# A block-sparse layer, two gated feed-forwards and a state-space mixer on one core: another order for the mask of the first stage and for the last phase of the mixer

## The chip, the core and the metric

The kernel runs on one core of a Trainium2 chip, as one launch. A core has a matrix engine (TensorE, PE in the profile, whose loads of stationary operands have a row of their own, PEld), VectorE (DVE), ScalarE (ACT), GpSimd (POOL) and SyncE (SP), which here only issues DMA transfers. Each engine works through its own list of instructions in order and waits for the others by semaphores. The metric is the device time of one execution in microseconds; lower is better.

## What is computed

1024 tokens (2 sequences of 512) of width 512, in float32, go through four residual layers. In each, `x` is normalised first:

```python
x = x + attn_a(layernorm(x), mask, weight, bias)      # block-sparse linear layer
x = x + ffn(layernorm(x), gate, up, down)             # integer weights, dequantised
x = x + attn_b(layernorm(x), in_proj, conv, ...)      # state-space mixer, 128 heads
x = x + ffn(layernorm(x), gate, up, down)

# attn_a: a block of 32x32 weights counts if any entry of its mask is set
bm  = mask.reshape(16, 32, 16, 32).sum(axis=(1, 3)) > 0
w   = (weight.reshape(16, 32, 16, 32) * bm[:, None, :, None]).reshape(512, 512)
out = einsum('bsk,nk->bsn', data, w) + bias

# attn_b, its end: y of all 8192 channels is normalised, gated and projected
var = mean(square(y), axis=-1)
y   = y * rsqrt(var + eps) * norm_w * silu(gate)
return y @ out_proj_w.T
```

Of the rest of the mixer only this matters here: a projection of each token into gates, channels and scores, a short convolution, a scan over chunks of 128 tokens, and the projection above.

## The kernel before

**Layout.** Tokens lie in 8 tiles of 128 (`x_sb[:, t, :]`, token on the partition, 512 wide). The normalised and turned input `xn_t` has the width on the partition, in 4 chunks `kc` of 128. `norm(t, True)` (line 110) issues the statistics of tile `t` (two VectorE instructions, L115 and L117) and a square root on ScalarE (L119); it returns a function which, called later, does the reciprocal and the offset on VectorE (L122, L126) and writes the normalised tile `tmp` on ScalarE (L127). `turn` (line 137) transposes such a tile by four TensorE instructions and copies it into `xn_t` on ScalarE (L143).

**Who sets the order.** `tc.manual_schedule` (line 1537) takes TensorE, ScalarE and VectorE as they stand in the code: what is written first runs first. The lists of POOL and SP are put in order by a planner from dependencies, priorities and its own estimates.

**First stage** (`block_sparse`, line 290). The weight comes in four chunks `wt[:, kc]` and the mask in four chunks `mk[:, kc]`. `masked(kc)` (line 322) is a generator in two parts. The look-up sums the mask over 32 columns on VectorE (`rows`, L325) and over 32 rows on TensorE, by a product with a block matrix (`pb`, L327). The masking compares that with zero on VectorE (`on`, L330) and multiplies the chunk of weights by it (L333), on VectorE for chunks 0 to 2 and on POOL for chunk 3. After some 20 warming products (`stir`), tiles 0 and 1 are normalised and turned, and their products run chunk by chunk in alternation (lines 358 to 364) with the look-up and the masking of the next chunk between them. The loop after that (line 371) takes tile after tile: POOL adds the bias to `x` (L372), TensorE multiplies, VectorE adds the product to `x` (L383), and the tile is normalised for the feed-forward.

**Mixer.** It works through the 8192 channels in 32 phases of two tiles of 128 channels. Each phase's projection is added into `acc`, which shares its memory with `x_sb`; the input is kept in DRAM (`x_d`) and read back into `xr`. Squares of `y` are summed into `sq_acc` by `squares` (line 947): ScalarE squares, POOL adds.

**Last phase** (lines 1456 to 1533). It finishes the scores and scans of the last two channel tiles and interleaves the start of the second feed-forward. `back_scores(k)` makes one set of scores (ScalarE and POOL); `flush` does the waiting multiplies by `gm` on VectorE (L900); `half_scan(units[2:], "proj")` is the TensorE part of the scan for the second sequence and `finish` its two VectorE instructions per channel tile (`y`, L939; `gt`, L942). `last_outs(t)` projects token tile `t`: four TensorE instructions (L956) and an addition on VectorE (L968), at once for tiles 0 to 3 and put off to the end (`adds`) for tiles 4 to 7. Tiles 0 to 3 need the first sequence alone; tiles 4 to 7 need `gt` of the second. `factors(b)` sums the squares of a sequence over the partitions on TensorE (`ms`, L1421) and forms the factor `rn` (L107, L108). `rest(t)` (line 1445) is `residual(t)`, which forms `acc * rn + xr` in one VectorE instruction (L1441), followed by `norm(t, True)`. Before the change, `ahead(t)` (line 1494) issues `rest(t + 1)` and then the normalised tile `t`. The second feed-forward starts with `pg` and `pu` (L486), which read all four turned tiles of the first sequence.

Of the kernel before, what the change touches and what calls it, by code (L numbers as in the profile page):

```python
# [11 lines left out]
ALU = mybir.AluOpType  # L12
AX = mybir.AxisListType

P = 128
# [5 lines left out]
KC = DIM // P  # L21
# [16 lines left out]
def kernel(  # L38
# [25 lines left out]
    nc = tc.nc  # L64
# [72 lines left out]
    def turn(normed):  # L137

        t, xn = normed
        pt = psum.tile([P, KC, P], F32, tag="tr", name="ln_tr")  # L140
        for kc in range(KC):
            nc.tensor.transpose(pt[:, kc, :], xn[:, kc * P : (kc + 1) * P], ident)
        nc.scalar.copy(xn_t[:, :, t * P : (t + 1) * P], pt)  # L143
# [85 lines left out]
    def stir(n):  # L229

        ps = psum.tile([P, P], F32, tag="tr", name="stir")
        for _ in range(n):
            nc.tensor.matmul(ps, lhsT=ones, rhs=ones, start=True, stop=True)
# [44 lines left out]
    def now(q_compute):  # L278
        q, compute = q_compute
        compute()  # L280
        return q

    def dequant_gate(s, scratch, third=False):
        return dequant_in(s, gate_w, gate_z, gate_s, scratch, third)

    def dequant_up(s, scratch, third=False):
        return dequant_in(s, up_w, up_z, up_s, scratch, third)


    def block_sparse():  # L290

        with tc.tile_pool(name="bs", bufs=1) as pool:

            def scratch(shape):
                return [pool.tile(shape, ty, name=nm, bufs=2) for nm, ty in (("wi", I32), ("zi", I32), ("sf", F32))]

            wt = pool.tile([P, KC, DIM], F32, name="wt")
            mk = pool.tile([P, KC, DIM], I32, name="mk")
            bias_b = pool.tile([P, DIM], F32, name="bias_b")

            def load_x(t):
                nc.sync.dma_start(x_sb[:, t, :], x_in[t * P : (t + 1) * P, :])

            for t in range(2):
                load_x(t)
            for kc in range(KC):
                nc.scalar.dma_start(mk[:, kc], mask_t[kc * P : (kc + 1) * P, :])
                nc.sync.dma_start(wt[:, kc], w_t[kc * P : (kc + 1) * P, :])

            nc.scalar.activation(small.tile([P, 1], F32, name="root"), eps, AF.Sqrt)  # L310
            for t in range(2, 5):
                load_x(t)
            nc.sync.dma_start(bias_b, bias.to_broadcast([P, DIM]))
            for t in range(5, NT):
                load_x(t)
            bd = pool.tile([P, P], F32, name="bd")
            nc.vector.memset(bd, 0.0)
            for i in range(4):
                nc.vector.memset(bd[32 * i : 32 * i + 32, 32 * i : 32 * i + 32], 1.0)
            NB = DIM // 32  # L320

            def masked(kc):

                rows = pool.tile([P, NB], F32, name="rows", bufs=2)
                nc.vector.tensor_reduce(rows, mk[:, kc].rearrange("p (b j) -> p b j", j=32), AX.X, ALU.add)  # L325
                pb = psum.tile([P, NB], F32, tag="yo", name="pb", bufs=3)
                nc.tensor.matmul(pb, lhsT=bd, rhs=rows, start=True, stop=True)  # L327
                yield
                on = pool.tile([P, NB], F32, name="on", bufs=2)
                nc.vector.tensor_scalar(on, pb, 0.0, None, ALU.is_gt)  # L330
                wv = wt[:, kc].rearrange("p (b j) -> p b j", j=32)
                eng = nc.gpsimd if kc == KC - 1 else nc.vector
                eng.tensor_tensor(wv, wv, on.unsqueeze(2).to_broadcast([P, NB, 32]), ALU.mult)  # L333
                yield

            def product(t, po, kc):
                nc.tensor.matmul(
                    po,
                    lhsT=xn_t[:, kc, t * P : (t + 1) * P],
                    rhs=wt[:, kc, :],  # L340
                    start=(kc == 0),
                    stop=(kc == KC - 1),
                )

            def bs_o():
                return psum.tile([P, DIM], F32, tag="proj", name="bs_o", bufs=3)


            stir(20)
            mask = [masked(kc) for kc in range(KC)]  # L350
            halves = [norm(t, True) for t in range(2)]
            normed = [h() for h in halves]
            next(mask[0])
            for n in normed:
                turn(n)
            next(mask[0])
            pos = [bs_o() for _ in range(2)]
            for kc in range(KC):
                product(0, pos[0], kc)
                if kc + 1 < KC:  # L360
                    next(mask[kc + 1])
                product(1, pos[1], kc)
                if kc + 1 < KC:
                    next(mask[kc + 1])
            ahead = norm(2, True)()
            half = norm(3, True)
            waiting = []
            half_f = None
            loaded = [dequant_gate(0, scratch), dequant_up(0, scratch)]
            first = []  # L370
            for t in range(NT):
                nc.gpsimd.tensor_add(x_sb[:, t, :], x_sb[:, t, :], bias_b)  # L372
                if t < 2:
                    po = pos[t]
                else:
                    po = bs_o()
                    for kc in range(KC):
                        product(t, po, kc)
                if t + 2 < NT:
                    turn(ahead)  # L380
                if t + 3 < NT:
                    ahead = half()
                nc.vector.tensor_add(x_sb[:, t, :], x_sb[:, t, :], po)  # L383
                if t + 4 < NT:
                    half = norm(t + 4, True)
                if half_f:
                    waiting.append(half_f())
                half_f = norm(t, True)
                if t in (4, 5):
                    first.append(now(loaded.pop(0)))  # L390
                if len(waiting) == 2:
                    turn(waiting.pop(0))
            waiting.append(half_f())
        return first, [lambda n=n: lambda: turn(n) for n in waiting]
# [274 lines left out]
    def mixer(waiting, step_args, loaded):  # L669

        with ExitStack() as st:
# [206 lines left out]
            def flush():  # L878
                for f in mults:
                    f()  # L880
                mults.clear()
# [274 lines left out]
            for ph in range(1, n_ph + 1):  # L1156
# [19 lines left out]
                def all_squares():  # L1176
                    for b, y in ys:
                        squares(b, y)
                    ys.clear()
# [9 lines left out]
                def back_scores(k):  # L1189
                    half_scores(k, c1, heads)  # L1190
# [227 lines left out]
            def factors(b):  # L1418
                ms = psum.tile([P, NCH], F32, tag="tr", name="ms")
                for c in range(NCH):  # L1420
                    nc.tensor.matmul(  # L1421
                        ms[:, c : c + 1],
                        lhsT=sq_acc[:, b, c * P : (c + 1) * P],
                        rhs=ones[:, 0:1],
                        start=True,
                        stop=True,
                    )
                rsqrt(rn[:, b * NCH : (b + 1) * NCH], ms, 1.0 / INTER)
# [16 lines left out]
            def rest(t):  # L1445
                residual(t)
                return norm(t, True)
# [3 lines left out]
            def last_outs(t):  # L1451

                tag = "proj" if t in (4, 6, 7) else "yo"
                out_project(n_ph - 1, [t], gts, wo_last, tag, None if t < NCH else adds)
# [31 lines left out]
            flush()  # L1486
            last_outs(1)
            back_scores(7)
            factors(0)
            last_outs(2)  # L1490
            flush()
            half = rest(0)

            def ahead(t):

                nonlocal half
                new = rest(t + 1)
                normed = half()
                half = new
                return normed  # L1500

            scans = half_scan(units[2:], "proj")
            normed = ahead(0)
            finish(scans)
            last_outs(3)
            turn(normed)
            normed = ahead(1)
            last_outs(4)
            turn(normed)
            normed = ahead(2)  # L1510
            last_outs(5)
            all_squares()
            turn(normed)
            normed = half()
            last_outs(6)
            turn(normed)
            last_outs(7)
            for f in adds:
                f()
            factors(1)  # L1520
# [3 lines left out]
            half = norm(NCH)  # L1524
# [101 lines left out]
```

## Time and profile before

| | us |
|---|---|
| median of 3 runs | 2304.89 (2302.44 to 2306.73) |
| the profiled execution, its own time | 2304.02 |
| its span, first to last instruction | 2302.3 |
| first stage, to the first product of the feed-forward (`pg`) | 0 to 47.4 |
| first feed-forward | 47.4 to about 314 |
| mixer | about 314 to 2039.6 |
| of it: last phase, from its first transposes | 1991.7 to 2039.6 |
| second feed-forward | 2039.6 to 2302.3 |

The profile is of one execution. "Busy" is time in which an engine works on an instruction; TensorE's instructions are pipelined and their ends are modelled, so that starts of successive ones say more than lengths. The chain of waits follows the work that ended last backwards to what released each step. Idle time of an engine that does not set the end costs nothing.

### The profile page before, as it was taken

The numbers are of one execution on the slowest core, as the hardware profiler recorded it, in microseconds if no ns is written. First come the engines' busy times: TensorE is split into PE (matmuls) and PEld (weight loads), VectorE is DVE, ScalarE is ACT, GpSimd is POOL, SyncE is SP. The second block draws the span as 40 slices with busy tenths as digits, with TensorE's granted clock in tenths as the row PEclk, the third lists the DMA queues.
The fourth block names the chain that finished last, engine by engine and source line by source line (L and its number), as shares of the span: only waits on it lengthen the run. The fifth ranks groups of instructions, "written<-read, shape, count | busy, mean of one in ns | idle before, by whom it ended". The sixth has DMA issues, their size and how long they took to land.

```text
span 2302.3 us, 30183 instructions
## 1 busy us (share of the span) xinstructions
PE 2242.4 (97%) x10704; PEld 1411.4 (61%) x10704; DVE 1805.7 (78%) x3042; ACT 1180.2 (51%) x2532; POOL 1243.9 (54%) x1206
## 2 busy tenths in 40 slices
PE   9999999999999999999999999999999999999999
PEld 5445865656665666666566656666666665544468
DVE  5456568888888888888888888888888888865553
ACT  4111056756666665666566656656655666631100
POOL 3765024656655666566556555664665665527620
PEclk9999999999999999999999999999999999999999
DMA  5563021222222222222221222221222322326600
GB/s 188 191 199 105 28 74 55 74 74 65 73 74 65 74 85 71 74 74 74 64 74 65 77 68 75 74 83 58 81 75 63 110 65 74 119 83 223 201 24 28
DMA packets 145783, 201.59 MB, mean 88 GB/s; under 512 B 7136, under 2 KB 92000, under 8 KB 145632
## 3 DMA queue, kind: packets, MB, share of 16 engines
q1 hardware_dynamic: 145056, 198.61, 27.1%
q8 instruction: 85, 1.39, 0.3%
q10 hardware_dynamic: 576, 1.05, 0.1%
q14 instruction: 66, 0.54, 0.1%
HBM read 194.91 MB, written 4.72 MB: 87 GB/s over the span
## 4 chain that ended last, share of the span: by engine, by line
PE 83%; DVE 14%; issue 2%; ACT 1%; DMA 1%; POOL 0%; ACTq 0%; SPq 0%; POOLq 0%; DVEq 0%
PE proj L185 29%; PE yo L185 17%; PE po L1020 10%; PE ffn_o L556 7%; DVE m L900 5%; DVE x_sb L1034 5%; PE py L919 4%; PE pst L848 4%; PE py L928 3%; PE x_tr L827 2%; PE po L956 2%; DVE gt L942 1%; PE pg L486 1%; PE pu L486 1%; DVE xc L734 1%
## 5 line engine op out<-in xcount | busy, mean ns | idle before, releaser
L906 POOL TENSOR_TENSOR ce<-ce,c_t 128x384 f32<-128x384 f32 x256 | 267.7, 1051 | 340.7 <-ACT ce L902 335.0
L185 PE MATMUL proj<-xn_t,w 128*128 128x512 f32 x824 | 384.6, 593 | 2.0 <-DVE gt L206 1.7
L892 ACT ACTIVATE m<-bc,acs 128x128 f32<-128x128 f32 x1024 | 324.9, 390 | 4.4 <-PE py L919 4.4
L185 PEld LDWEIGHTS proj<-xn_t,w 128*128 128x128 f32 x824 | 153.0, 190 | 146.4 <-issue 137.7
L1034 DVE TENSOR_TENSOR x_sb<-x_sb,po 128x512 f32<-128x512 f32 x340 | 228.9, 679 | 9.5 <-PE po L1020 4.9
L171 POOL TENSOR_TENSOR ws<-w 128x256 f32<-128x256 f32 x96 | 72.9, 760 | 292.2 <-DMA w<-in_win_t_dram 242.1
L734 DVE SCALAR_TENSOR_TENSOR xc<-proj,cw,xc 128x511 f32<-128x511 f32 (+2 forms) x288 | 214.6, 746 | 6.6
L900 DVE TENSOR_TENSOR m<-m,gm 128x512 f32<-128x512 f32 x256 | 218.6, 876 | 0.0
L919 PE MATMUL py<-m,x_dt 128*64 128x128 f32 x2048 | 194.1, 278 | 13.7 <-DVE m L900 13.6
L949 POOL TENSOR_TENSOR sq_acc<-sq_acc,y 128x512 f32<-128x512 f32 x128 | 178.4, 1400 | 46.5 <-ACT y L948 43.8
L185 PE MATMUL proj<-tq,ws 128*128 128x512 f32 x432 | 199.2, 592 | 0.0
L1020 PE MATMUL po<-wo,gt 128*128 128x256 f32 x696 | 177.0, 384 | 0.0
L919 PEld LDWEIGHTS py<-m,x_dt 128*64 128x64 f32 x2048 | 135.8, 137 | 49.0 <-issue 25.8
L899 ACT ACTIVATE m<-m 128x512 f32<-128x512 f32 x256 | 161.3, 630 | 7.4
L185 PE MATMUL yo<-xn_t,w 128*128 128x512 f32 x328 | 151.7, 595 | 12.8 <-DVE tmp L206 12.8
L928 PE MATMUL py<-ce,state 128*64 128x128 f32 x1536 | 157.6, 274 | 0.0
L862 DVE SCALAR_TENSOR_TENSOR state<-state,e_last,pst 128x64 f32<-128x64 f32 x512 | 107.0, 276 | 60.2 <-ACT state L857 57.7
L185 PE MATMUL yo<-tq,ws 128*128 128x512 f32 x336 | 153.4, 599 | 0.2 <-ACT acs L714 0.2
L1020 PEld LDWEIGHTS po<-wo,gt 128*128 128x128 f32 x696 | 125.5, 190 | 30.9 <-issue 7.1
L749 ACT ACTIVATE xc<-xc 128x512 f32<-128x512 f32 x128 | 72.5, 621 | 134.3 <-DVE xc L734 133.9
L731 ACT ACTIVATE xc<-proj,cb,cw 128x512 f32<-128x512 f32 x96 | 74.4, 778 | 129.5 <-DVE proj L225 76.6
L942 DVE SCALAR_TENSOR_TENSOR gt<-y,nw,gt 128x512 f32<-128x512 f32 x128 | 137.1, 1071 | 2.5
(228 smaller groups left out, 4559.5 us busy)
## 6 DMA issues: line engine op xcount, KB each, us to landing
bc<-acs_d SPq DMA_DIRECT2D x128, 512.0 KB, 3.8
w<-in_win_t_dram SPq DMA_DIRECT2D x64, 512.0 KB, 3.8
wo<-in_wo_t_dram SPq DMA_DIRECT2D x31, 512.0 KB, 5.0
wi<-in_down_w_dram SPq DMA_DIRECT2D x14, 512.0 KB, 4.0
zi<-in_down_z_dram SPq DMA_DIRECT2D x14, 512.0 KB, 4.8
sf<-in_down_s_dram SPq DMA_DIRECT2D x14, 512.0 KB, 4.2
wi<-in_gate_w_dram SPq DMA_DIRECT2D x13, 512.0 KB, 4.3
zi<-in_gate_z_dram SPq DMA_DIRECT2D x13, 512.0 KB, 5.2
```

Source lines behind the costliest of these rows:

```text
L185: nc.tensor.matmul(ps, lhsT=a[:, kc, :], rhs=b[:, kc, :], start=(start and kc == 0), stop=(stop and kc == KH - 1), skip_group_check=True,)
L556: nc.tensor.matmul(ps, lhsT=a[:, k, :], rhs=b(k), start=(start and k == 0), stop=(stop and k == KF - 1), skip_group_check=True,)
L734: nc.vector.scalar_tensor_tensor(dst[:, s:], ps[:, : SEQ - s], cw[:, t, 3 - s : 4 - s], dst[:, s:], ALU.mult, ALU.add)
L892: nc.scalar.activation(m[:, c, :], bc[:, hh, c * P : (c + 1) * P], AF.Relu, bias=acs[:, t, h : h + 1], scale=-1.0,)
L899: nc.scalar.activation(m, m, AF.Exp, scale=-1.0)
L900: mults.append(lambda: nc.vector.tensor_mul(m, m, shared[b][2]))
L906: nc.gpsimd.tensor_mul(ce, ce, c_t[:, P:].rearrange("p (c l) -> p c l", l=P))
L919: nc.tensor.matmul(py[hh * HD : (hh + 1) * HD, c * P : (c + 1) * P], lhsT=x_dt[:, c, hh, :], rhs=m[:, c, :], start=True, stop=(c == 0),)
L928: nc.tensor.matmul(py[hh * HD : (hh + 1) * HD, c * P : (c + 1) * P], lhsT=state[:, c - 1, hh, :], rhs=ce[:, c - 1, :], start=False, stop=True,
L949: nc.gpsimd.tensor_add(sq_acc[:, b, :], sq_acc[:, b, :], y)
L1020: nc.tensor.matmul(banks[k][:, c, :], lhsT=a[:, t], rhs=b, start=(start and c == 0), stop=stop, skip_group_check=True,)
L1034: nc.vector.tensor_add(q, q, banks[k])
```

## The change

In the first stage, the look-ups of chunks 0 and 1 are issued ahead of the turns of tiles 0 and 1, and that of chunk `kc + 2` ahead of the products of chunk `kc`; the maskings stay between the two products of the chunk before. The masking of chunk 3 is done by VectorE like the others.

In the last phase, the waiting multiply (`flush`) and `rest(0)` come ahead of the projection of tile 2, `rest(1)` stays behind the issue of the scan; the normalised tile 1 is written ahead of the residuals of tiles 2 and 3; the squares come ahead of the projection of tile 4; the two residuals are issued together, ahead of the projection of tile 5; and the turns of tiles 1, 2 and 3 each stand one projection later than before.

```diff
@@ -329,8 +329,7 @@
                 on = pool.tile([P, NB], F32, name="on", bufs=2)
                 nc.vector.tensor_scalar(on, pb, 0.0, None, ALU.is_gt)
                 wv = wt[:, kc].rearrange("p (b j) -> p b j", j=32)
-                eng = nc.gpsimd if kc == KC - 1 else nc.vector
-                eng.tensor_tensor(wv, wv, on.unsqueeze(2).to_broadcast([P, NB, 32]), ALU.mult)
+                nc.vector.tensor_tensor(wv, wv, on.unsqueeze(2).to_broadcast([P, NB, 32]), ALU.mult)
                 yield
 
             def product(t, po, kc):
@@ -350,18 +349,20 @@
             mask = [masked(kc) for kc in range(KC)]
             halves = [norm(t, True) for t in range(2)]
             normed = [h() for h in halves]
+
             next(mask[0])
+            next(mask[1])
             for n in normed:
                 turn(n)
             next(mask[0])
             pos = [bs_o() for _ in range(2)]
             for kc in range(KC):
+                if kc + 2 < KC:
+                    next(mask[kc + 2])
                 product(0, pos[0], kc)
                 if kc + 1 < KC:
                     next(mask[kc + 1])
                 product(1, pos[1], kc)
-                if kc + 1 < KC:
-                    next(mask[kc + 1])
             ahead = norm(2, True)()
             half = norm(3, True)
             waiting = []
@@ -1486,35 +1487,27 @@
             flush()
             last_outs(1)
             back_scores(7)
+            flush()
             factors(0)
+            first_rest = rest(0)
             last_outs(2)
-            flush()
-            half = rest(0)
-
-            def ahead(t):
-
-                nonlocal half
-                new = rest(t + 1)
-                normed = half()
-                half = new
-                return normed
-
             scans = half_scan(units[2:], "proj")
-            normed = ahead(0)
+            second_rest = rest(1)
+            normed = first_rest()
             finish(scans)
             last_outs(3)
             turn(normed)
-            normed = ahead(1)
+            normed = second_rest()
+            all_squares()
             last_outs(4)
+            halves = [rest(2), rest(3)]
+            last_outs(5)
             turn(normed)
-            normed = ahead(2)
-            last_outs(5)
-            all_squares()
-            turn(normed)
-            normed = half()
+            normed = [h() for h in halves]
             last_outs(6)
-            turn(normed)
+            turn(normed[0])
             last_outs(7)
+            turn(normed[1])
             for f in adds:
                 f()
             factors(1)
```

## The prediction, made before the changed kernel was run

> **What bounds the kernel now.** First the page's busy row and its chain, for the bound of the whole; then the chain of waits and the timeline in the two stretches that the change touches, 8 to 23 us and 2016 to 2040 us; then the windows, for the granted clock there.
>
> ```profile
> PE 2242.4 (97%) x10704; PEld 1411.4 (61%) x10704; DVE 1805.7 (78%) x3042; ACT 1180.2 (51%) x2532; POOL 1243.9 (54%) x1206
> PE 83%; DVE 14%; issue 2%; ACT 1%; DMA 1%; POOL 0%; ACTq 0%; SPq 0%; POOLq 0%; DVEq 0%
> ```
>
> TensorE is the bound, and its order is written by hand. So what is worth anything is time in which PE stands still, and a stall removed early should reach the end unless a later wait hangs on something other than PE. The first stretch, as a timeline (start, length, engine, line, operation; in brackets the idle before and who ended it):
>
> ```profile
> 14.60 2.49 POOL L372 TENSOR_TENSOR x_sb<-x_sb,bias_b 128x512 f32<-128x512 f32 x2 [12.61 <-DMA bias_b<-in_bias_dram]
> ...
> 17.04 1.05 POOL L333 TENSOR_TENSOR wt<-wt,on 128x512 f32<-128x512 f32 x1
> ...
> 18.14 0.30 PEld L337 LDWEIGHTS bs_o<-wt,xn_t 128*128 128x128 f32 x2 [2.48 <-POOL wt L333]
> ```
>
> The masking of the last chunk runs on POOL behind two bias additions, which wait for the bias (landed at 14.43). Its look-up was done at 15.75; PE has it at 18.14. The earlier chunks stall PE too: the look-up's reduction, PE sum, comparison and multiply of a chunk follow each other between two products. The last phase, as the chain of waits (start, length, what):
>
> ```profile
> 2027.15 0.60 DVE x_sb L968
> 2027.74 0.67 DVE x_sb L1441
> 2028.44 0.70 DVE stats L115
> 2029.17 0.18 DVE mv L117
> 2029.35 0.06 DVE rstd L122
> 2029.43 0.23 DVE off L126
> 2029.66 0.03 issue
> 2029.68 0.82 ACT tmp L127
> 2030.51 0.04 issue
> 2030.55 0.98 PE ln_tr L142 x4
> 2031.53 3.08 PE po L956 x4
> ```
>
> PE ran out at 2028.06 and waits 2.5 us for VectorE to do tile 2's residual and statistics and only then tile 1's scale, because each normalised tile is written one step after its statistics. The last two rows are too long (0.98 for four transposes that take 0.44 elsewhere, 3.08 for products that take 1.72), and the windows of half a microsecond say why (length, busy of PE, PEld, DVE, ACT, POOL, then the granted clock):
>
> ```profile
> 2030.00:2030.50 0.50, 0.00 (x0) 0.00 (x0) 0.47 (x2) 0.50 (x1) 0.00 (x0) 1.00 0.00 0
> 2030.50:2031.00 0.50, 0.45 (x3) 0.45 (x4) 0.50 (x1) 0.00 (x0) 0.00 (x0) 0.74 0.00 0
> 2031.00:2031.50 0.50, 0.50 (x4) 0.50 (x3) 0.43 (x4) 0.00 (x0) 0.00 (x0) 0.50 0.00 0
> ...
> 2034.00:2034.50 0.50, 0.50 (x3) 0.16 (x2) 0.00 (x0) 0.09 (x1) 0.50 (x1) 0.85 0.00 0
> ```
>
> The clock is halved from about 2030.75 to 2034.1, which costs half of those 3.35 us, 1.7 us.
>
> **First stage, step by step.** Added: nothing but order, and 0.69 us of VectorE (the multiply row: 692 ns each on three chunks) for 1.05 us of POOL. No DMA moves; SP's and ACT's loads keep their order, and the mask chunks landed at 4.7, 6.1, 7.7 and 8.7 us, the weight chunks by 10.0, before their new uses. VectorE's spacings from its rows: reduction to next 0.70, comparison to multiply 0.21, multiply to next 0.61. From the first reduction at 7.32 that gives: reduction of chunk 1 at 8.02, comparison and multiply of chunk 0 at 8.70 and 8.91, reduction 2 at 9.52, chunk 1 masked 10.41 to 11.10, reduction 3 at 11.02, chunk 2 masked 11.91 to 12.60, chunk 3 (after its PE sum) 13.0 to 13.7.
>
> The wait that this adds: PE's sum for chunk 1 now stands ahead of the turns of tiles 0 and 1 and waits for reduction 1. It can start at 9.04, so the transposes start at 9.19 in place of 8.49, ACT's copies at 9.86, and the first product, behind the sum of chunk 2 as well, at 10.68 in place of 9.80: 0.9 us lost. Then PE need not wait: eight products at 0.857 (four tiles of 3.43 us for four products) and one sum at 0.14 end at 17.68. Every chunk is masked before its turn (the closest, chunk 2: 12.60 for 14.25). Tile 2's normalised tile, 1.71 us from the start of its statistics (15.67 to 17.38) and 0.81 long, starts from 13.61 and is ready at 16.13, so the turn follows at once, at 17.68 in place of 19.96. **2.28 us gained.** The two bias additions still start at 14.6 and end at 17.1, in time for the first residual sum at 17.15. Everything after this hangs on PE: from 22.5 to 2020 the rows of PE follow each other, and the loads of the next stage are issued when buffers come free, so they move along. I take the 2.28 us to the end.
>
> **Last phase, step by step** (times within 2000). Moved on VectorE: one product of scores (L900, 0.60) from behind the third sum to before `rn`, residual 1 and its statistics stay, residual 2 and 3 with statistics go behind tile 1's scale. On ACT the two squares (1.14 together) and on POOL their two sums (1.3 each) come before the statistics of 2 and 3. No DMA is among them. VectorE idled from 18.40 to 19.49 for PE's sum of tile 2; the moved product and residual 0 now fill that. Spacings from the rows: sum 0.60, residual 0.78, statistics 0.73, aggregate 0.10, reciprocal and offset 0.30 together, `y` 0.77, `gt` 0.67. So: residual 0 at 19.06, sum 2 at 20.67, residual 1 at 21.27, offset 0 at 23.05, `gt` at 23.95 and 25.40 (before: 24.95 and 26.40), sum 3 at 26.07, offset 1 at 26.83, residual 2 at 26.97, residual 3 at 28.58.
>
> PE: tile 3's product ends at 24.31 as now; turn 0 finds its tile (ready 24.11) and takes 0.43; tile 4's first half runs to 25.60, the second waits for `gt` until 26.20 (0.6 stays); tile 5 runs to 28.78; turn 1 finds its tile (ready 27.89); tile 6 runs from 29.21 to 30.93. What is late next is turn 2: ACT must do both later statistics' roots, then copy 1, then tile 2. If nothing interferes, tile 2 is ready at 31.9, turn 2 is at 31.95, tile 7 at 32.38, turn 3 at 34.10, the squares' sum at 34.53 and the next stage at 35.34, against 39.57: 4.23 us.
>
> Here a rule speaks against the change. The row first: the `gt` product of the same form as a residual takes 0.75 alone, and this when a POOL operation is running:
>
> ```profile
> 2009.15 0.99 POOL L906 TENSOR_TENSOR ce<-ce,c_t 128x384 f32<-128x384 f32 x1 [4.49 <-ACT ce L902]
> ...
> 2009.36 1.33 DVE L942 SCALAR_TENSOR_TENSOR gt<-y,nw,gt 128x512 f32<-128x512 f32 x1
> ```
>
> It ended 0.55 after POOL let go at 10.14. The Trainium skill (SBUF — State Buffer, "shared port pair") says that a VectorE operation with two SBUF inputs and a GpSimd one exclude each other for the whole instruction. The first square, earlier now, ends at 28.40 and POOL starts its 1.28 us sum at 28.47, 0.1 before residual 3 at 28.58. By the row's own excess the price is 0.58; by the lock residual 3 waits until 29.75 and ends at 30.30 in place of 29.33, 0.97 late; were it first, POOL would wait and the price is nothing. I take the lock, with POOL first, since the row fits it to the hundredth. Then tile 2 is ready at 32.87, turn 2 at 32.92, tile 7 at 33.35, turn 3 at 35.07, the sum at 35.50, the next stage at 36.31. **3.26 us gained.**
>
> The second rule: the skill's TensorE page (TensorE: Matmul & The Clock Gate, Part 1) has the clock halved after an idle window of some 3.4 us. PE's longest idle here was 2.2 us and the clock fell all the same: in the 3.4 us before it fell PE did 0.7 us of products, and in the 3.4 us before those 1.4 us, without a fall. So the trace makes it a matter of too little work, with the decision between 0.7 and 1.4. In the new order the thinnest stretch of that length, ending with turn 2, holds 1.0 us of products and a turn; only about a third of the positions of a window would catch it. So I count no half clock and gain the 1.7 us. By the rule as it stands the gap was not the reason, the half clock could stay, and the sum would be 3.8 in place of 5.5.
>
> The next stage hangs on the squares' sum and on residuals 4 to 7, which follow it by the same distance as now. Sum: 2.28 + 3.26 = **5.5 us**. The profiled execution took 2304.02 (span 2302.3 and 1.7 around it) and would take 2298.5; it lay 0.87 under the median of 2304.89, so the forecast is **2299.4**.
>
> **Rivals.**
> - No collision of residual 3 with POOL (a margin of 0.1 us decides): 6.5 us, 2298.4. Chance 0.25, against 0.40 for the forecast.
> - The clock falls again, in the gap before turn 2 (2.0 us of idling, see above), or at 8.5 to 10.7 in the first stage, where PE now has only transposes and sums: 1.7 us lost, 2301.1; both, 2302.8. Nothing in the trace fixes where the windows of the gate lie. Chance 0.22.
> - Slower: the orders of POOL and SP are a planner's, as the mask put behind bias additions that come after it in the code shows. If earlier due times make it place a load or a `ce` product worse in the repeated phases of the mixer (SP's `bc` loads alone wait 1023.6 us for ACT's `ce`), the price comes some 30 times: 0.18 us a phase eats the gain, and at 0.3 the time is 2304.9 - 5.5 + 9 = 2308.4. Against it: nothing in these phases changed, and a shift of all of them alike has no reason to reorder them. Chance 0.13, with the case that gains vanish in some other wait.
>
> **How the numbers follow.** Medians of this kernel scatter by a microsecond or two (2302.44 to 2306.73), so I spread each case by 1.2 us. 0.2%, or 4.6 us, is about what a measurement of this kernel tells from no change; faster than 2300.3 then: 0.77 of the forecast's case, 0.94 of the first rival, a quarter of the second, together 0.60; within 0.2% 0.27; slower 0.13. The range, 2296.8 to 2302.6, holds the first two cases and most of the third.
>
> **What would show it.** The turn of tile 2 at about 17.7 us with no LDWEIGHTS idle over 0.5 us from 11 to 20; chunk 3's multiply on DVE at 0.69. At the end: PE idle before turns 0 and 1 gone, 1 to 2 us before turn 2, residual 3 at 0.75 or 1.7 us, no window at clock 0.50, some 13.7 us in place of 17.0 from tile 3's product to the first `pg`. I am wrong if the repeated phases (some 49 us each) change in length, or the first product starts later than 11 us.

## The result and the profile after

| | before | after |
|---|---|---|
| median, us | 2303.24 (2301.29 to 2306.73, 9 runs) | 2297.92 (2297.01 to 2299.91, 9 runs) |
| the profiled execution, its own time | 2304.02 | 2297.01 |
| its span | 2302.3 | 2295.3 |
| turn of tile 2 in the first stage | 19.96 | 17.24 |
| tile 3's projection (`po`) in the last phase | 2022.59 | 2018.85 |
| first `pg` of the second feed-forward | 2039.57 | 2032.55 |

The ratio of after to before is 0.9975, with a 95% interval of 0.9965 to 0.9985: 5.3 us faster by the medians, where 5.5 were forecast. The time forecast, 2299.4, was reckoned from a median of three runs that lay 1.65 above the median of nine.

The busy row and the chain of the page after:

```profile
PE 2236.9 (97%) x10704; PEld 1408.4 (61%) x10704; DVE 1806.8 (79%) x3043; ACT 1179.9 (51%) x2532; POOL 1241.6 (54%) x1205
PE 83%; DVE 15%; issue 1%; ACT 1%; DMA 0%; SPq 0%; ACTq 0%; DVEq 0%
```

Nothing new bounds the kernel: one instruction has gone from POOL to VectorE, and PE carries the chain as before. PE's busy time fell by 5.5 us although it does the same 10704 instructions. Apart from the very end, the execution before had three windows of half clock and the one after has one, which accounts for up to 3.4 of it; the rest is not resolved, the ends of PE's instructions being modelled.

The first stage, in the timeline after (start, length, engine, line, operation; in brackets the idle before and who ended it):

```profile
10.07 1.96 PE L336 MATMUL bs_o<-wt,xn_t 128*128 128x512 f32 x4
...
12.01 5.40 PE L336 MATMUL bs_o<-wt,xn_t 128*128 128x512 f32 x12
...
12.41 0.69 DVE L332 TENSOR_TENSOR wt<-wt,on 128x512 f32<-128x512 f32 x1
...
14.70 3.73 POOL L373 TENSOR_TENSOR x_sb<-x_sb,bias_b 128x512 f32<-128x512 f32 x3 [12.72 <-DMA bias_b<-in_bias_dram]
...
17.24 0.60 PE L142 MATMUL ln_tr<-ident,tmp 128*128 128x128 f32 x4
```

Twelve product instructions follow each other without a gap behind the first four; the waits of PE for a masking are gone. Chunk 3 is masked at 12.41, more than two microseconds before the bias lands and POOL begins to add it at 14.70. The turn of tile 2 stands at 17.24, 2.72 earlier than before.

The last phase, as the chain of waits after (start, length, what):

```profile
2022.37 0.60 DVE x_sb L969
...
2023.29 0.67 DVE x_sb L1442
...
2023.98 0.71 DVE stats L115
...
2024.89 1.67 DVE x_sb L1442
...
2026.58 0.71 DVE stats L115
...
2027.73 0.57 ACT xn_t L143
2028.30 0.72 ACT tmp L127
...
2029.06 0.66 PE ln_tr L142 x4
2029.72 1.72 PE po L957 x4
2031.44 0.44 PE ln_tr L142 x4
2031.88 0.79 PE ms L1422 x8
2032.66 3.59 PE pg L487 x8
```

One residual takes 0.67 in the chain, the next 1.67. `po` is back at 1.72 and the last four transposes at 0.44, the full clock. Beside the long residual, that of tile 3, the timeline of the same kernel has POOL's two additions of squares (`sq_acc`):

```profile
2024.73 1.27 POOL L950 TENSOR_TENSOR sq_acc<-sq_acc,y 128x512 f32<-128x512 f32 x1 [11.50 <-ACT y L949]
2024.81 1.74 DVE L1442 SCALAR_TENSOR_TENSOR x_sb<-x_sb,rn,xr 128x512 f32<-128x512 f32 x1
2026.08 1.59 POOL L950 TENSOR_TENSOR sq_acc<-sq_acc,y 128x512 f32<-128x512 f32 x1
```

POOL was first by 0.08 us. Its first addition ends at 2026.00, the residual at 2026.55.

**Where the 7.0 us between the two profiled executions came from.** The same pieces of PE's chain, before less after: 2.73 at 76 us and still 2.70 at 346; 3.92 at 500; 3.60 at 1777; 3.74 at 1980; 7.02 at `pg`. So the first stage gave 2.72, the last phase 3.28 (its stretch from tile 3's projection to `pg` went from 16.98 to 13.70), and about 1.0 belongs to neither: it appears at about 430, where the execution before had a window of half clock and the one after had not. The medians are only 5.3 apart, so this single pair of spans flatters the change.

### The profile page after: what moved, and what is told of

It is laid out like the page before. It is cut to its first block, busy times and chain, and to the rows that moved or that the text cites. A ratio compares the mean times of both kernels' runs of the same rounds, so it can differ in the third digit from the quotient of the medians.

```text
span 2295.3 us, 30182 instructions
## 1 busy us (share of the span) xinstructions
PE 2236.9 (97%) x10704; PEld 1408.4 (61%) x10704; DVE 1806.8 (79%) x3043; ACT 1179.9 (51%) x2532; POOL 1241.6 (54%) x1205
## 3 DMA queue, kind: packets, MB, share of 16 engines
q8 instruction: 85, 1.39, 0.2%
## 4 chain that ended last, share of the span: by engine, by line
PE 83%; DVE 15%; issue 1%; ACT 1%; DMA 0%; SPq 0%; ACTq 0%; DVEq 0%
PE proj L185 29%; PE yo L185 17%; PE po L1021 10%; PE ffn_o L557 7%; DVE m L901 5%; DVE x_sb L1035 5%; PE py L920 4%; PE pst L849 4%; PE py L929 3%; PE x_tr L828 2%; PE po L957 2%; DVE gt L943 2%; PE pg L487 1%; PE bs_o L336 1%; PE pu L487 1%
```

## The experiments

In what follows "stretch" is the time from tile 3's projection to the first `pg`, and "turn" is the turn of tile 2 in the first stage; both are read from the timeline of each kernel.

### Each part alone

The first part of the change on the kernel before (the last phase untouched), and the second part on the kernel before (the first stage untouched).

> The kernel before with the first-stage part of the change alone. My theory (the two parts act on separate stalls of TensorE and add up): the turn of tile 2 starts at 17.2 us as in the changed kernel (19.96 before), the next stage's first product 2.7 us earlier than before, and from tile 3's projection to the first product of the second feed-forward still about 17.0 us if the clock is halved there again, 15.3 if not. Time about 2.7 us under the kernel before. Rival (an early gain is swallowed by some later wait in the mixer): the first stage is 2.7 us shorter and the last phase starts at the old time, 2022.6 us.

> The kernel before with the last-phase part of the change alone. My theory: turn of tile 2 at 19.96 us as before; from tile 3's projection to the first product of the second feed-forward 13.7 us in place of 17.0; time about 3.3 us under the kernel before, and with the other part alone the sum is about 6 us. Rival (the last phase gains only because the first stage shifted it against the windows of the clock gate): about 15.3 us or more for that stretch.

| | turn | stretch | median, us | ratio to before |
|---|---|---|---|---|
| before | 19.96 | 16.98 | 2303.48 | |
| first part alone | 17.47 | 16.99 | 2300.09 | 0.9985 (0.9978 to 0.9992) |
| second part alone | 19.89 | 13.69 | 2300.36 | 0.9989 (0.9982 to 0.9995) |
| both parts, repeated on another chip (before, there: 2303.52) | 17.66 | 13.69 | 2297.60 | 0.9976 (0.9968 to 0.9985) |

Each part moves its own number and leaves the other alone. The two ratios multiply to 0.9974, which is within the interval of both parts together, so nothing here speaks against independent parts. Both gains reach the end: with the first part alone tile 3's projection starts at 2019.69 in place of 2022.59, and neither interval includes 1. The repetition:

> The changed kernel once more, as the measure for the two orders below on the same chip. From tile 3's projection to the first product of the second feed-forward 13.7 us; residual 3 at 1.7 us on VectorE, because POOL's sum of squares started 0.1 us before it.

### Is it the engine, or the order of the look-ups?

Two edits sit in the first stage. Each alone, on the kernel before:

```diff
-                eng = nc.gpsimd if kc == KC - 1 else nc.vector
-                eng.tensor_tensor(wv, wv, ...)
+                nc.vector.tensor_tensor(wv, wv, ...)
```

> The kernel before with chunk 3 masked by VectorE and nothing else. My theory: the multiply runs at 15.8 to 16.5 us, its products follow, but tile 2's statistics are 0.7 us later on VectorE, so the turn of tile 2 waits for its normalised tile and starts at about 18.9 us (19.96 before, 17.24 with both): a gain of 1.0 of the 2.7 us. Rival (the queue on POOL was all of the loss): the turn at 17.3 us.

```diff
             next(mask[0])
+            next(mask[1])
...
             for kc in range(KC):
+                if kc + 2 < KC:
+                    next(mask[kc + 2])
                 product(0, pos[0], kc)
                 if kc + 1 < KC:
                     next(mask[kc + 1])
                 product(1, pos[1], kc)
-                if kc + 1 < KC:
-                    next(mask[kc + 1])
```

> The kernel before with the look-ups a chunk ahead and chunk 3 still masked by POOL. My theory: the products of chunks 0 to 2 end some 2 us earlier, but POOL still masks chunk 3 behind two bias additions, from 17.0 to 18.1 us, and the turn of tile 2 starts at about 19.9 us: no gain. Rival (the two edits of the first stage add up, 1.0 and 1.7 us): the turn at about 18.3 us.

The timeline with VectorE alone changed:

```profile
13.97 2.49 POOL L371 TENSOR_TENSOR x_sb<-x_sb,bias_b 128x512 f32<-128x512 f32 x2 [11.99 <-DMA bias_b<-in_bias_dram]
...
15.64 1.37 DVE L332 TENSOR_TENSOR wt<-wt,on 128x512 f32<-128x512 f32 x1
...
19.51 0.66 PE L142 MATMUL ln_tr<-ident,tmp 128*128 128x128 f32 x4 [0.46 <-ACT tmp L127]
```

and with the look-ups alone changed:

```profile
15.15 2.48 POOL L374 TENSOR_TENSOR x_sb<-x_sb,bias_b 128x512 f32<-128x512 f32 x2 [13.18 <-DMA bias_b<-in_bias_dram]
17.60 1.04 POOL L333 TENSOR_TENSOR wt<-wt,on 128x512 f32<-128x512 f32 x1
...
18.69 0.30 PEld L337 LDWEIGHTS bs_o<-wt,xn_t 128*128 128x128 f32 x2 [3.21 <-POOL wt L333]
```

On VectorE without the early look-up, the masking of chunk 3 comes at 15.64, while POOL adds the bias. It doesn't take 0.69 but 1.37: POOL's second addition ends at 16.46, the masking 0.55 later. That is the same 0.55 which the prediction read at the `gt` product. The turn waits for its normalised tile, as expected, but it is at 19.51: a gain of 0.45 where 1.06 was expected, because the masking under POOL's addition had been put at its length alone. With the early look-up alone, POOL still does the masking, and still behind the two bias additions; here the bias landed 0.55 later than in the execution before, the turn is at 20.51, and the gain is nothing.

So the two edits are worth 0.45 and nothing apart, and 2.3 to 2.7 together. For the look-ups alone the theory (no gain) held; both rivals, the queue on POOL as the whole loss and two shares that add up, fall. The early look-up lets the masking be ready for 12.41, ahead of the bias; on VectorE it can run then, while POOL's list has two bias additions in front of it. Whether POOL would do as well with its masking put ahead of them was not tried. The single times (2302.66 and 2303.87) lie within the scatter of the kernel before and settle nothing by themselves.

### Does residual 3 lose to POOL's sum of squares?

On the changed kernel, the squares between the two residuals:

```diff
-            all_squares()
             last_outs(4)
-            halves = [rest(2), rest(3)]
+            halves = [rest(2)]
+            all_squares()
+            halves.append(rest(3))
```

> The changed kernel with the two squares issued between the residuals of tiles 2 and 3. My theory (VectorE and POOL exclude each other for a whole instruction, and who starts first wins): residual 3 starts before POOL's first sum and takes 0.75 us in place of 1.74, POOL's first sum waits instead, the turn of tile 2 comes 0.95 us earlier and the stretch takes 12.75 us in place of 13.7. Rival (residual 3 is slow for another reason, such as its reading of the transferred tile or both engines sharing bandwidth): it still takes 1.2 us or more and the stretch stays over 13.3 us.

```profile
2024.19 0.72 DVE L1442 SCALAR_TENSOR_TENSOR x_sb<-x_sb,rn,xr 128x512 f32<-128x512 f32 x1
...
2025.20 2.63 POOL L950 TENSOR_TENSOR sq_acc<-sq_acc,y 128x512 f32<-128x512 f32 x2 [12.58 <-ACT y L949]
```

In this timeline POOL starts after residual 3 has ended, the residual takes 0.72 in place of 1.74, and the stretch is 12.68 in place of 13.70. The collision costs 1.02 of stretch, and the theory without a collision falls. That the two engines merely share bandwidth does not fit either: POOL's first addition took 1.27 during the collision and takes 1.27 here without one, so only VectorE lost time. That POOL waits when VectorE is first was not put to the test, as POOL's input comes too late here. The nearest to it is POOL's second addition in the kernel after, which begins at 2026.08 beside the residual and takes 1.59, against 1.28 here.

### Does the wait before turn 2 have to be there?

```diff
             last_outs(6)
-            turn(normed[0])
             last_outs(7)
+            turn(normed[0])
             turn(normed[1])
```

> The changed kernel with the turns of tiles 2 and 3 both behind the projection of tile 7. My theory: the projection fills the 1.6 us in which TensorE waited for tile 2; the stretch takes 12.2 us, residual 3 stays at 1.74 us. Rival (the copies of the turned tiles on ScalarE, now all at the end, become the wait of the next stage): 13 us or more, with the first product of the next stage waiting for a copy.

Stretch 12.52, residual 3 still 1.74. Tile 7's products fill what PE waited for tile 2, but 0.3 of the expectation is missing. The timeline has the eight transposes at 1.36 there, and at 1.04 in the two kernels below, where residual 3 is not delayed: with tile 2's wait filled, the delay of residual 3 is felt at tile 3. With both edits:

> The changed kernel with both edits, squares between the residuals and the turns of tiles 2 and 3 last. My theory: the stretch takes 11.8 us, 1.9 us less than in the changed kernel, and the time is under that of both kernels, by about 1.9 us of the changed one. Rival: the two edits remove the same wait, so the stretch is 12.2 us as with the turns alone.

The stretch came to 12.36, not 11.8, and that is nearer to the rival. The gains of the two edits do overlap (1.02 and 1.18 alone, 1.34 together). But residual 3 took 0.72 here and the eight transposes 1.04, so its price was gone; something else had taken its place. The timeline of this kernel shows what:

```profile
2030.84 1.04 PE L142 MATMUL ln_tr<-ident,tmp 128*128 128x128 f32 x8
...
2031.48 1.07 ACT L143 COPY xn_t<-ln_tr 128x512 f32<-128x512 f32 x2 [0.92 <-PE ln_tr L142]
...
2032.21 1.02 PE L1422 MATMUL ms<-ones,sq_acc 128*128 128x1 f32 x8 [0.33 <-ACT xn_t L143]
```

The squares' sum `ms` waits 0.33 us for ScalarE's copy of tile 2, whose data it doesn't read. Both take their buffer in PSUM (`psum` in the code, where the products of this kernel go) under the tag `tr`, which has two; with two turns in a row just ahead, `ms` must wait until the first is copied out. In the next kernel it takes its buffer from another tag:

```diff
-                ms = psum.tile([P, NCH], F32, tag="tr", name="ms")
+                ms = psum.tile([P, NCH], F32, tag="yo" if b else "tr", name="ms", bufs=3 if b else 2)
```

> The kernel with both edits, and with the last sum of squares put into another group of PSUM banks (that of the projections), so that it no longer waits for the copy of tile 2's turn to free its bank. My theory (in the kernel with both edits this bank was the wait that took the place of tile 2's normalisation, 0.3 to 0.6 us): the stretch from tile 3's projection to the next stage takes 11.8 us in place of 12.36, the squares' sum follows the turns at once, and the time is about 1.9 us under the changed kernel's. Rival (the copy of tile 3 on ScalarE is the later wait in any case): 12.3 us, with the next stage's first product waiting for the copy.

```profile
2029.94 1.04 PE L142 MATMUL ln_tr<-ident,tmp 128*128 128x128 f32 x8
...
2030.82 0.95 PE L1422 MATMUL ms<-ones,sq_acc 128*128 128x1 f32 x8
...
2031.70 2.84 PE L487 MATMUL pg<-xn_t,w 128*128 128x512 f32 x6
```

The bracket is gone from `ms`, which starts 0.88 behind the first transpose in place of 1.37, and the stretch is 11.88: the wait was for the buffer. Timed:

| | stretch | median, us | ratio to the kernel before |
|---|---|---|---|
| the change, repeated | 13.69 | 2297.60 | 0.9976 (0.9968 to 0.9985) |
| with both edits | 12.36 | 2296.40 | 0.9967 (0.9956 to 0.9978) |
| and the other buffer | 11.88 | 2295.25 | 0.9966 (0.9954 to 0.9978) |

Both beat the kernel before for certain. That they beat the change is shown by the stretches; the intervals of the times overlap.

### Was the early multiply worth anything?

On the changed kernel, `flush` back behind tile 2's projection, so that VectorE idles ahead of residual 0 as before:

```diff
             back_scores(7)
-            flush()
             factors(0)
             first_rest = rest(0)
             last_outs(2)
+            flush()
```

> The changed kernel with the multiply of the last scores moved back behind tile 2's addition on VectorE; residual 0 stays early. My theory (VectorE's idle time is filled by residual 0 in either order, and what the multiply's place decides is only when the second scan can start): the second scan starts 0.4 us later, tile 3's projection too, but the gating products of VectorE and so everything behind them stay: from the first product of the scan to the next stage 16.9 us as in the changed kernel, from tile 3's projection to the next stage 13.3 in place of 13.7. Rival (the early multiply carries 1.0 us of the gain): 17.9 us from the scan's first product.

The stretch is 13.19, but its start moved. From the scan's first product to `pg` it is 16.90 here (2016.22 to 2033.12) and 16.91 after (2015.64 to 2032.55), and in both that product starts 1.90 behind tile 2's projection. The multiply's place buys nothing: residual 0 fills the idle time as well.

### Was the half clock one of too little work?

On the kernel before, ten products of no use (two instructions each in the profile) in the gap ahead of turn 1:

```diff
             last_outs(4)
+            stir(10)
             turn(normed)
```

> The kernel before with ten extra products of constants on TensorE (their result is not used) between the projection of tile 4 and the turn of tile 1, where TensorE idles for 2.5 us. They take about 2.1 us and should not delay the turn. My theory (the clock is halved after a window with too little TensorE work, here because of this gap, and the half clock costs about 1.6 us): no half clock from the turn on, four transposes 0.44 us and a projection 1.72 us apart, and the stretch from tile 3's projection to the first product of the second feed-forward takes 15.3 us in place of 17.0. Rival (the half clock has another cause, such as the thin stretch from 2024 to 2028): the clock still falls and the stretch stays at 17.0 us.

The stretch is 15.45, and there is no half clock in the last phase; the transposes that took 0.98 take 0.66. The turn still comes 3.35 behind the second half of tile 4's projection, as before, so the filling delayed nothing. (The single time, 2304.64 against 2303.31 of one run of the kernel before, does not show the gain; this execution lost time to a half clock in its first stage, where its turn of tile 2 came at 21.01.) One run without it is not yet a proof, since the kernel with VectorE alone changed, whose last phase is that of before, had none either (stretch 15.44). What decides is the window. In the thirteen profiled executions half clock lasts 3.41 us at a time, twice it lasts 6.83, and the last one is cut off by the end of the profile. Within an execution all of them start on one grid of 3.41 us (before, 429.89, 1928.34 and 2030.74 are whole multiples of 3.4133 apart). Cut on its own grid, the stirred kernel reads (columns: window, length, then busy and count of PE, PEld, DVE, ACT, POOL, granted clock, DMA share, GB/s):

```profile
15.85:19.26 3.41, 1.38 (x4) 0.49 (x3) 2.03 (x8) 1.40 (x3) 3.41 (x4) 1.00 1.09 353
19.26:22.67 3.41, 2.81 (x7) 1.21 (x5) 2.23 (x5) 0.57 (x2) 0.23 (x1) 0.50 1.04 330
...
2029.71:2033.13 3.42, 3.42 (x26) 2.80 (x25) 3.28 (x8) 1.11 (x2) 0.00 (x0) 1.00 0.00 0
```

The gap lay inside 2029.71 to 2033.13, and PE was busy in all of it. The timeline tells what of that was stir:

```profile
2030.33 2.39 PE L233 MATMUL stir<-ones 128*128 128x128 f32 x20
2032.72 0.66 PE L142 MATMUL ln_tr<-ident,tmp 128*128 128x128 f32 x4
```

Without it the window would have held some 1.2 us of work (the projection up to its modelled end at 2030.50, and 0.4 from 2032.72). Every window with so little, in all thirteen executions, was followed by half clock, as the first two rows show in the first stage of the same kernel, where 1.38 is followed by 0.50.

So of the 3.28 us by which the stretch became shorter, 1.54 (16.98 to 15.44) were half clock and 1.74 were waits. Of the four executions with the last phase of before and nothing added, three had the half clock there (16.98, 16.99 and 16.99) and one had not.

## The prediction, point by point

**The bound and the path to the end: right.** PE's order carries gains from 23 us to the end: 2.73 at 76 us is still 2.70 at 346, and the first part alone is 3.4 us faster by its median. The order of POOL's and SP's lists is the same before and after but for the masking that left POOL, so the slower rival had no ground. Of the signs that the prediction listed one missed: PEld idles 1.62 at 19.23, ahead of tile 3's turn. PE waits 1.39 there for the normalised tile, as it did before the change at 21.95, so this is a wait that the change leaves.

**First stage: right, the size 0.2 too small.** Over the eight profiled executions that hold this first stage the turn comes at 17.24 to 17.66, mean 17.46; 17.68 was forecast. The misjudged term is the loss at the start. The prediction had the first product at 10.68; after, it stands at 10.07. Of this, 0.22 is that the first reduction began at 7.10 in place of 7.32 in this execution. From a reduction to PE's sum it took 0.34 of idling, from a row where PE was busy with warming products, and after it is nearer 0.05; and it spaced reductions by 0.70 where they follow by 0.59. From the first product to the turn it then counted 7.00, and 7.17 was measured. What the prediction did not see is how the gain arises: it summed the order and the engine as parts of one schedule, and they work only together. The margin it listed last, chunk 3 masked by 13.7, has the bias addition close behind (13.97 to 15.15 in the executions shown), and beyond that the masking costs twice as much.

**Last phase: right term by term.** Take 3.74 off its times, by which the phase came earlier: POOL's sum at 24.73 (it started at 24.73), residual 3 at 24.84 (24.81), turn 2 at 29.18 (29.06), `pg` at 32.57 (32.55). Residual 3 was said to take 1.7 under the lock and took 1.74. By the starts of PE's instructions, as the prediction reckoned, PE stands still for 1.8 before turn 2, where 2.0 was forecast; the trace, with modelled ends, counts 1.64. The margin by which POOL is first was 0.1 in the prediction and is 0.07 or 0.08 in all five kept executions with this order of the residuals, so the collision was no accident of one run. One term bought nothing: the earlier multiply, which the prediction named with residual 0 as filler of VectorE's idle time, and residual 0 suffices.

**The lock against the row's own excess.** The lock made residual 3 0.97 late; by the excess of the `gt` row it was 0.58. Measured: 1.02 of the stretch. The Trainium skill (SBUF — State Buffer, Terms, "shared port pair") says that the loser blocks for the whole instruction of the other. The measurement agrees: what sets the price is how much of POOL's instruction is left when VectorE's arrives, 0.78 us for `gt` and 1.19 for residual 3. But the row did not fit the rule "to the hundredth". An operation of 0.75 that starts when POOL lets go would end 0.75 later, and all three cases, `gt`, the masking and residual 3, end 0.55 later, 0.14 to 0.2 sooner than by the rule. Why stays open.

**The half clock: the choice was right, the chance attached to it too high for this stretch.** The prediction set the decision between 0.7 and 1.4 us of products in a window that ended where the clock fell. Its 0.7 and 1.4 leave out the transposes and count the products by their starts. Cut on the grid, with all that PE did, the window before the fall holds 1.19 and the one before that 2.51, and other windows put the decision between 1.4 and 1.7. These windows are on the grids of four kernels; before:

```profile
426.47:429.89 3.42, 1.59 (x14) 0.97 (x9) 3.35 (x13) 2.91 (x8) 0.33 (x1) 1.00 0.00 0
429.89:433.30 3.41, 3.41 (x8) 2.72 (x9) 2.55 (x4) 3.38 (x11) 2.00 (x2) 0.50 0.46 154
...
2027.33:2030.74 3.41, 1.19 (x4) 0.36 (x5) 3.27 (x8) 1.11 (x2) 0.00 (x0) 1.00 0.00 0
2030.74:2034.15 3.41, 3.41 (x8) 1.82 (x8) 1.71 (x7) 2.52 (x5) 0.51 (x1) 0.50 0.00 0
```

after:

```profile
424.33:427.75 3.42, 1.58 (x7) 1.07 (x7) 3.35 (x13) 3.39 (x9) 0.40 (x1) 1.00 0.00 0
427.75:431.16 3.41, 3.41 (x18) 3.00 (x17) 3.41 (x6) 3.35 (x10) 1.60 (x2) 1.00 0.45 154
...
2025.19:2028.60 3.41, 2.23 (x9) 0.93 (x7) 3.21 (x8) 1.24 (x4) 2.40 (x2) 1.00 0.00 0
2028.60:2032.01 3.41, 2.95 (x16) 1.95 (x16) 1.99 (x4) 1.80 (x4) 0.00 (x0) 1.00 0.00 0
```

with VectorE alone changed:

```profile
2028.97:2032.39 3.42, 1.67 (x7) 1.07 (x8) 2.74 (x10) 2.08 (x5) 0.00 (x0) 1.00 0.00 0
2032.39:2035.80 3.41, 3.41 (x15) 1.70 (x14) 1.85 (x5) 2.73 (x5) 2.23 (x2) 1.00 0.00 0
```

with both edits and the other buffer:

```profile
424.76:428.18 3.42, 1.69 (x10) 1.10 (x7) 3.35 (x13) 3.27 (x9) 0.32 (x2) 1.00 0.00 0
428.18:431.59 3.41, 3.41 (x10) 2.70 (x9) 2.48 (x5) 3.35 (x11) 2.17 (x2) 0.50 0.50 154
```

The window behind 1.19 has the clock at 0.50, the one behind 1.67 has it at 1.00, and the one behind 1.69 at 0.50 again. After the change the two windows that share the gap hold 2.23 and 2.95. The idle time before turn 2 is 1.64, so wherever the grid lies a window there keeps some 1.8 us of work, more than in any window at full clock that brought half clock; the prediction had reckoned with 1.4 there, and so with a third of the positions. The four kept executions with this gap, each with a grid of its own, have no half clock in the last phase. The Trainium skill (TensorE: Matmul & The Clock Gate, Part 1) has the clock halved after an idle window of 3413 ns that runs freely, whenever the kernel starts. The length and the free running agree with the grid here; that the window must be idle doesn't, since PE worked for 1.59 us of one in the kernel before and the clock fell. The prediction also said that nothing in the trace fixes the windows. The trace did: the half clock at 429.89 gives the grid of that execution. It doesn't give the next one's, whose grid lies elsewhere.

The forecast's case, 5.5 us with the collision and without half clock, is what happened. That the medians agree within 0.2 us is in part luck: the forecast took the half clock of one execution of the kernel before as given, and it is there in three of four. The rivals fell: no collision (residual 3 took 1.74), a new half clock (none in the first or the last stage after), another order of POOL and SP (it is the same).

## What to carry to other kernels

When a wait is shortened by moving an instruction, look what else holds the port, the buffer or the engine at its new time: the same masking cost 0.69 at 12.4 us and 1.37 at 15.6, and the same sum `ms` waited 0.33 us for a buffer whose data it did not need. Compare stretches between two fixed pieces of work rather than spans, since a single execution can win or lose 1.5 us by where a window of the clock falls. A gap of the limiting engine costs more than its length if it leaves too little work in a window, so filling it with later work that is ready may pay twice: the turns one projection later did both here.

## What was not expected of the hardware

- **A window of half clock follows a window with little work, not only one of idleness.** By the traces of all thirteen executions, cut on their own grids, half clock followed every window at full clock in which PE was busy for 1.39 us or less, and none with 1.70 or more. Between, from 1.52 to 1.69, five windows brought it and 57 did not, so that the busy time, with its modelled ends, doesn't draw a sharp line. The longest idle stretch of PE in the last phase before was 2.2 us. In two executions half clock went on for a second window, though PE was busy for 2.2 and 2.3 us of the first one, at half clock.
- **The position of the grid differs from execution to execution.** The last phase of the kernel before took 16.98 us with a half clock and 15.44 without, in the same code. Part of the scatter of its times (2301.29 to 2306.73) may come from that; this was not tested.
- **A start 0.1 us earlier decides a microsecond.** POOL at 2024.73 against VectorE at 2024.81 cost residual 3 1.02 us. Residual 3 ended 0.55 after POOL let go, as did the masking on VectorE that POOL's additions caught in the first stage, and the `gt` product.
